# Key-cache gathers in rows of 4 KB instead of 8 KB and 16 KB

## The chip, the cores and the metric

The kernel runs on one core of a Trainium2 chip. The metric is the device time of one execution in microseconds (us). Before the change the median of 5 runs is 1200.76 us (1194.84 to 1205.26). One more execution was recorded by the hardware profiler: it took 1201.02 us, of which 1199.2 us lie between its first and its last instruction (the span). All steps are worked out from that execution.

## The reference, cut to what matters

Four layers are added to `x` (64 sequences of 64 tokens, 512 wide, float32), each with a residual. The third is attention over a paged key and value cache; it holds everything that the change touches. For sequence `b`, token `t` stands at position `pos = kv_lens[b] + t`, and sees the 256 positions up to its own:

```
blk = take_along_axis(block_tables, pos // 16, axis=1)
k_blocks = k_blocks.at[blk, :, pos % 16, :].set(k)      # blocks of [4 heads, 16 positions, 64]
k_all = k_blocks[block_tables]                          # per sequence: its blocks in order
scores = einsum('bghtd,bgsd->bghts', qg, k_all) * SCALE
allowed = (kpos <= pos) & (kpos > pos - 256)
p = softmax(where(allowed, scores, -inf)); o = einsum(p, v_all); out = o @ Wo.T
```

`qg` are the queries, 2 heads to each of the 4 key heads. The new keys are written into blocks of the shared cache before they are read, and the block tables are drawn at random, so a block that one sequence writes may be read by others. The first layer multiplies each sequence by its own 64x64 matrix, the second and fourth are linear layers with low-rank adapters by sequence.

## The kernel before

**What a sequence needs.** A sequence's window touches at most NR = 21 blocks of 16 positions. The kernel takes four sequences at a time: 4 x 21 = 84 blocks, one block to a partition. There are 16 such quadruples, `q` = 0 to 15.

**Two sources of a key block.** Blocks come first from the cache as it was (`kblk`, 16 KB a block, stored head by head: [4 heads, 16 positions, 64]), and then blocks that the kernel itself has written are put over them. The written blocks lie in a scratch tensor `pk` in HBM, 320 rows of 16 KB, stored position by position ([16 positions, 4 heads, 64]); the first stage fills it through `put_rows` (scatters at line 71). `ik_old` and `ik_new` (lines 119 and 120 of the kernel, filled in `gather_indices`, lines 573 to 576) hold the row numbers of both, for each of the 84 partitions and 16 quadruples. Where a block was not written, the number in `ik_new` is out of bounds, and the gather leaves the partition as it is.

**The steps of a key block.** All gathers are issued by POOL through the helper at line 65.
- `k_load(q, h)` (line 148): gathers two heads of the 84 cache blocks into `kt`, 8 KB a row; two calls make a quadruple.
- `k_copy(q, o4)` (line 154): ACT or DVE copies every fourth position from `kt` to `k2`, turning the order to position by position. Four calls make a quadruple.
- `k_patch(q)` (line 161): one gather of 16 KB rows from `pk` over `k2`.
- `k_turn(q, gp, o4)` (lines 169 to 184): PE transposes the positions `4*oq + o4`, oq = 0 to 3, of two heads into one PSUM bank (line 175); DVE or ACT copies it to `kT_mem` (lines 183, 184). Eight calls make a quadruple.

**Values.** `v_load(b)` issues four gathers of 92 rows of 1 KB into `vs_mem`, `v_copy(b)` copies them on ACT into `vt_mem` (line 197), `v_patch(b)` gathers written blocks over them (92 rows of 4 KB, bounded), and `v_share(b)` moves some of the rows by three DMAs from SP (line 208).

**The stages.** In the first stage (to about 450 us) the tokens go through layers one and two, keys, values and queries are made, and the new rows are scattered; the last quarter of the queries is left for the second stage. The second stage has 128 steps, 8 for a quadruple: two for each sequence, one for each half of the heads (`gp`). The order on every engine is the order of the program, written out by hand. A round of 8 steps (`i = s % 8`) issues on POOL: at even `i` four value gathers for sequence b+3; at odd `i` the value patch for b+2, which waits for that sequence's `v_copy` at the end of the step before; at `i` = 1 the key patch of the next quadruple; at `i` = 2 and 3 the cache gathers of the one after it. PE makes the first `k_turn` of the next quadruple at the end of step 3 and the other seven in steps 4 to 7. `k_copy` for the quadruple after it runs at `i` = 5, 6, 7 on DVE and at `i` = 0 of the next round on ACT. In the first round POOL also normalizes the queries that were left over (lines 242, 243, 248), and PE transposes them (line 283). Line 1059 is the product with Wo, lines 1067 to 1086 the fourth layer, line 983 the scores, line 1025 the transposes of the probabilities, line 1041 the product with the values.

Before the second stage, at `n == NTILE`, the program issues `k_patch(0)`, `v_patch(0)` and `v_patch(1)` on POOL, and query products of POOL behind them; `k_load(0, .)` and `k_load(1, .)` stand among the scatters of the first stage.

```
if i == 1:
    k_patch(q + 1)
if i in (2, 3):
    k_load(q + 2, i - 2)
```

Of the kernel before, what the change touches and what calls it, by code (L numbers as in the profile page):

```python
# [11 lines left out]
I32 = mybir.dt.int32  # L12
AF = mybir.ActivationFunctionType
ALU = mybir.AluOpType
# [4 lines left out]
P = 128  # L19
B, T, D = 64, 64, 512  # L20
# [3 lines left out]
NB_TAB = 257  # L24
# [3 lines left out]
NH, NG = 8, 4  # L28
# [3 lines left out]
NR = 21  # L32
NW = 5
W0 = NR - NW
NWR = B * NW
# [15 lines left out]
def kernel(  # L51
# [9 lines left out]
    V, S, G, PE, DMA = nc.vector, nc.scalar, nc.gpsimd, nc.tensor, nc.sync  # L61

    def gather(dst, src, idx, bound=None):
        more = {} if bound is None else dict(bounds_check=bound, oob_is_err=False)
        G.indirect_dma_start(  # L65
            out=dst, out_offset=None, in_=src,
            in_offset=bass.IndirectOffsetOnAxis(ap=idx, axis=0), **more,
        )
# [10 lines left out]

    k_halves = kblk.rearrange("n (h g) o d -> (n h) (g o d)", h=2)
    k_rows = kblk.rearrange("n g o d -> n (g o d)")
    v_blocks = vblk.rearrange("n g o d -> n (g o d)")
    v_rows = vblk.rearrange("n g (q o) d -> (n g q) (o d)", q=4)
# [2 lines left out]
    pk = dram.tile([NWR, ROW], F32, name="pk", tag="pk")  # L88
# [4 lines left out]
    def ctile(shape, dt, name, pool=const):  # L93
        return pool.tile(shape, dt, name=name, tag=name)
# [14 lines left out]
    woT_sb = ctile([P, 4, D], F32, "woT_sb")  # L109
# [6 lines left out]
    cen = ctile([P, B], F32, "cen")  # L116
    edge = ctile([P, 1], F32, "edge")
    lowb = ctile([P, B], F32, "lowb")
    ik_old = ctile([4 * NR, 2, 16], I32, "ik_old")
    ik_new = ctile([4 * NR, 16], I32, "ik_new")  # L120
    iv_old = ctile([NV, B, NG], I32, "iv_old")
    iv_new = ctile([NV, B], I32, "iv_new")
    iod_f = iod.rearrange("p o q j -> p (o q j)")
# [7 lines left out]
    kt = ctile([P, NG, BLK, HD], F32, "kt")  # L131
    k2 = ctile([P, BLK, NG, HD], F32, "k2")
# [8 lines left out]
    def bank(pool, name):  # L141
        return pool.tile([P, 512], F32, name=name, tag="b")

    NP = 4 * NR
# [3 lines left out]
    def k_load(q, h):  # L148

        if q < B // 4:  # L150
            gather(kt[:NP, 2 * h : 2 * h + 2].rearrange("p g o d -> p (g o d)"), k_halves,
                   ik_old[:, h, q : q + 1])

    def k_copy(q, o4):

# [2 lines left out]
                k2[:NP].rearrange("p (oq o) g d -> p oq o g d", o=4)[:, :, o4],  # L158
                kt[:NP].rearrange("p g (oq o) d -> p oq o g d", o=4)[:, :, o4])

    def k_patch(q):

        if q < B // 4:
            gather(k2[:NP].rearrange("p o g d -> p (o g d)"), pk, ik_new[:, q : q + 1], NWR - 1)

    def kT(q, gp):
        return kT_mem[q % 2][:, gp].rearrange("p (b o c i) -> p b o c i", b=4, o=3, c=4)
# [46 lines left out]
    def queries(n):  # L214

        return n - LQ if n < NTILE - 4 else -1 if n < NTILE else n - 4 - LQ
# [77 lines left out]
    with ExitStack() as one:  # L294
# [4 lines left out]
        def t1(shape, dt, name):  # L299
            return ctile(shape, dt, name, c1)  # L300
# [41 lines left out]
                        for i in range(2))  # L342
        kvb_i = t1([P, B], I32, "kvb_i")
        kvp_i = t1([P, 1], I32, "kvp_i")
        cond_i = t1([P, B], I32, "cond_i")
        ad1_i = t1([P, B], I32, "ad1_i")
        ad3_i = t1([P, B], I32, "ad3_i")
        tab_i = woT_sb[:, 2, :NB_TAB].bitcast(I32)
        sc1b = t1([P, 4], F32, "sc1b")
        sc3b = t1([P, 8], F32, "sc3b")  # L350
        pcol = t1([P, 1], F32, "pcol")
# [212 lines left out]
        def gather_indices(part):  # L564

            ps = bank(psO, f"ps_idx{part}")
            lhs, rhs, m, n = ((ix["lhs"].rearrange("p b j -> p (b j)"), ix["hi"], 4 * NR, 16)
                              if part < 2 else
                              (ix["lhsv"].rearrange("p c i -> p (c i)")[:, :NV], ident2, NV, B))
            o = ps[:m, :n]  # L570
            PE.matmul(o, lhsT=lhs, rhs=rhs, start=True, stop=True)
            if part == 0:
                for h in range(2):
                    V.tensor_scalar(ik_old[:, h], o, 2.0, float(h), ALU.mult, ALU.add)
            elif part == 1:
                V.tensor_copy(ik_new, o)
            elif part == 3:
                V.tensor_scalar(iv_new, o, 4.0, ix["oq"], ALU.mult, ALU.add)
            else:
                for g in range(NG):  # L580
                    V.tensor_scalar(iv_old[:, :, g], o, 16.0, ix["oqg"][:, g : g + 1],
                                    ALU.mult, ALU.add)
# [212 lines left out]
        def first_parts(s):  # L795

            if s >= NGRP:
                return [lambda: None] * 4

            def part0():  # L800
                for i in range(4):
                    mix(4 * s + i)
                ranks1(s)

            def part1():
                scale1(s)
                layer1(s, 0)

            def part3():
                layer1(s, 2)  # L810
                layer1(s, 3)

            return [part0, part1, lambda: layer1(s, 1), part3]
# [68 lines left out]
        for n in range(NLAST):  # L882
            if n % 4 == 0:
                parts = first_parts(n // 4 + 1)
            w_load0(n + 12)
            x2_load(queries(n + 2))
            if 1 <= n <= NTILE:
                new_rows(n - 1)
            if n != NTILE:
                norm_q(queries(n - 1))()  # L890
            lag = 4 if n < 20 else 3 if n < 22 else 2 if n < 24 else 1
            while done["p"] <= min(n - lag, NTILE - 1):
                put_rows(done["p"])
                done["p"] += 1
            if n == NTILE:
                k_patch(0)
                v_patch(0)
                v_patch(1)
                norm_q(queries(n - 1))()
            product_q(queries(n), psP)  # L900
            if n % 4:
                x_load0(n + 8)
            if n in (14, 16, 18, 20):
                gather_indices((n - 14) // 2)
            if n < NTILE:
                parts[n % 4]()
            if n % 4 == 0:
                x_load0(n + 8)
            if n == 1:
                written_rows()  # L910
                places()
            if n in (1, 2):
                for o4 in (0, 1):
                    fill_copy(2 * (n - 1) + o4)
            if n == 2:
                fill_store(pv)
            if n >= 2:
                winners(n + 1 + max(0, (n - 6) // 4))
            if 2 <= n < 8:
                zero_rows((pk, pv)[n % 2], n // 2 - 1)  # L920
            if n in (13, 15, 17, 19):
                index_lists((n - 13) // 2)
            if n % 4 == 3:
                mixers(n // 4 + 2)
            if 5 <= n < 10:
                late_inputs(n - 5)
            if 14 <= n < 18:
                positions(n - 14)
            if n == 19:
                adapters(ad3_i, sc3b, 8, mask3)  # L930
                middles()
            if n == 21:
                residual3()
                G.memset(sm_mem, 0.0)
            turn_q(queries(n - 5 if n == NTILE else n - 2 if n != NTILE - 3 else -1), psO)
            if n < NTILE:
                product_kv(n)
            if n in (NTILE - 13, NTILE - 12):
                k_load(0, n - (NTILE - 13))
            if n in (NTILE - 11, NTILE - 9):  # L940
                v_load((n - (NTILE - 11)) // 2)
            if n in (NTILE - 7, NTILE - 5):
                v_copy((n - (NTILE - 7)) // 2)
            if NTILE - 8 <= n < NTILE - 4:
                k_copy(0, n - (NTILE - 8))
            if n in (NTILE - 3, NTILE - 2):
                k_load(1, n - (NTILE - 3))
            if n == NTILE - 4:
                v_load(2)
# [167 lines left out]
    for s, (q, b, gp) in enumerate(steps):  # L1117
        i = s % 8
        turn1, turn2 = turns.get(i, (None, None))
        if i == 0 and q:  # L1120
            x_load(q)
        if i == 2:
            q_load(q + 1)
        if gp == 0:
            v_load(b + 3)
        else:
            v_share(b + 1)
            v_patch(b + 2)
        if i == 1:
            k_patch(q + 1)  # L1130
        if i in (2, 3):
            k_load(q + 2, i - 2)
        scores(s + 1)
        turn_p(s)
        if 0 < s < 16:
            turn_q(nq + s - 2, psO)
        if turn1:
            k_turn(q + 1, *turn1)
        maxima(s + 1)
        keep_p(s)  # L1140
        exponentials(s + 1)
        second = norm_q(nq + s if q < 2 else -1)
        if parts:
            parts.pop(0)()
        if q < 2:
            product_q(nq + s + 1, psM)
            x2_load(nq + s + 3)
        shares(s + 1)
        second()
        if gp:  # L1150
            window(b + 2)
        po = values(s)
        if turn2:
            k_turn(q + 1, *turn2)
        keep_o(s, po)
        if gp == 0:
            v_copy(b + 2)
        if i == 0:
            k_copy(q + 1, 3)
        elif i > 4:  # L1160
            k_copy(q + 2, i - 5)
        if i == 7:
            parts += last_parts(q)
# [53 lines left out]
```

## Time and profile before

| what | before |
|---|---|
| median of 5 runs (lowest to highest) | 1200.76 us (1194.84 to 1205.26) |
| the profiled execution | 1201.02 us |
| its span | 1199.2 us |
| granted TensorE clock, mean | 0.976 |
| PE / DVE / ACT / POOL busy | 1100.0 / 753.4 / 571.4 / 614.2 us |
| key patches, `k<-pk,ik_new` | 16, 1.01 us of POOL each |
| cache gathers, `kt<-in_kblk_dram,ik_old` | 32, 0.95 us (median) of POOL each |
| PE's idle time that a key patch ended | 15.0 us in 13 places |

PE is TensorE's matmuls, PEld its weight loads, DVE VectorE, ACT ScalarE, POOL GpSimd, SP SyncE. In a row of the timeline stand the start, the duration, the engine, the line, the operation, what it writes and reads (`out<-in`), the count, and in brackets the engine's idle time before it with what ended that. A gather's row on POOL is the time in which POOL makes its descriptors; when the data has landed is read from the updates of the gather's semaphore, and from whoever waits for it.

### The profile page before, as it was taken

How to read it: one execution, taken by the hardware profiler on the slowest of the kernel's cores; microseconds unless marked ns; L12 is line 12 of the kernel's file. 1: busy time of each engine (PE TensorE's matmuls, PEld its weight loads, DVE VectorE, ACT ScalarE, POOL GpSimd, SP SyncE). 2: the span in 40 equal slices, each digit the busy share in tenths (PEclk: the TensorE clock that was granted, in tenths of full speed). 3: DMA queues.
4: the chain of work that ended last, by engine and by line, in shares of the span. 5: the costliest groups of instructions: out<-in, count | busy, mean ns of one | idle time of the engine just before them, and what ended most of it. 6: DMA issues, size and time to landing. Idle time of an engine off the chain costs nothing.

```text
span 1199.2 us, 17686 instructions
## 1 busy us (share of the span) xinstructions
PE 1100.0 (92%) x5622; PEld 639.2 (53%) x5622; DVE 753.4 (63%) x2313; ACT 571.4 (48%) x1472; POOL 614.2 (51%) x601
## 2 busy tenths in 40 slices
PE   4998899999899986888999989999999999999998
PEld 4444444444444433445566556656656665665665
DVE  3675445756666683797666656666766676666561
ACT  1332222232224333555566656656666665666551
POOL 3153231333362262688666666667656666655620
PEclk9999999999899997898999999999999999999999
DMA  8366623132432364454665556457556755766420
GB/s 261 114 254 225 228 82 99 57 125 81 150 111 78 95 174 117 115 140 130 140 153 149 132 131 157 135 133 167 144 136 151 168 133 138 160 142 138 100 65 36
DMA packets 129821, 163.20 MB, mean 136 GB/s; under 512 B 58080, under 2 KB 96892, under 8 KB 125546
## 3 DMA queue, kind: packets, MB, share of 16 engines
q0 software_dynamic: 63872, 85.04, 29.4%
q1 hardware_dynamic: 46416, 53.89, 14.8%
q10 hardware_dynamic: 19440, 23.15, 5.7%
q8 instruction: 45, 0.74, 0.3%
q14 instruction: 48, 0.39, 0.1%
HBM read 139.66 MB, written 50.33 MB: 158 GB/s over the span
## 4 chain that ended last, share of the span: by engine, by line
PE 61%; DVE 11%; DMA 10%; ACT 5%; issue 5%; POOL 3%; ACTq 1%; SPq 0%; POOLq 0%; DVEq 0%
PE pso L1059 7%; PE pp L1025 6%; PE psc L983 6%; PE po L1041 6%; PE q L263 5%; PE ps L787 5%; PE psy L1084 5%; PE psy L1078 5%; PE kv L820 5%; DMA k<-pk,ik_new 4%; PE psk L175 3%; PE psxa L1067 2%; PE psy L1086 2%; DMA pv<-vt_mem,zidx 2%; PE ps L789 2%
## 5 line engine op out<-in xcount | busy, mean ns | idle before, releaser
L65 POOL DMA_INDIRECT vs_mem<-in_vblk_dram,iv_old x256 | 309.6, 1209 | 78.1 <-issue 67.6
L1009 ACT ACTIVATE sm_mem<-sm_mem,mn 128x336 f32<-128x336 f32 x256 | 145.6, 574 | 32.9 <-DVE mn L999 31.8
L65 POOL DMA_INDIRECT vt_mem<-pv,iv_new x64 | 80.1, 1252 | 135.7 <-ACT vt_mem L197 77.8
L999 DVE CUSTOM_DVE_ANT_0 sm_mem<-psc,pen 128x336 f32<-128x336 f32 x256 | 118.7, 500 | 16.4 <-PE psc L983 14.7
L1059 PE MATMUL pso<-oT,woT_sb 128*128 128x256 f32 x512 | 123.3, 385 | 0.0
L1041 PEld LDWEIGHTS po<-pT,vt_mem 124*64 124x64 f32 x1536 | 82.6, 136 | 75.4 <-ACT sm_mem L1009 54.2
L263 PE MATMUL q<-wq_sb,x2q 128*128 128x512 f32 x256 | 120.3, 615 | 0.0
L983 PE MATMUL psc<-kT_mem,qs 64*128 64x336 f32 x512 | 108.7, 500 | 10.7 <-DVE kT_mem L184 10.7
L787 PE MATMUL ps<-kT_mem,kT_mem 128*128 128x512 f32 x256 | 117.0, 600 | 0.6 <-PE ps_fill L493 0.6
L1041 PE MATMUL po<-pT,vt_mem 124*64 124x128 f32 x1536 | 113.7, 281 | 3.7 <-ACT pT L1032 3.7
L1025 PE MATMUL pp<-ident,sm_mem 128*124 128x128 f32 x768 | 114.0, 284 | 2.3 <-DVE sm_mem L1017 1.6
L1017 DVE TENSOR_SCALAR sm_mem<-sm_mem,rsum 128x336 f32<-128x336 f32 x256 | 110.3, 431 | 9.1
L820 PE MATMUL kv<-wkv_sb,xr 128*128 128x512 f32 x256 | 115.5, 595 | 0.4 <-ACT va L828 0.4
L1025 PEld LDWEIGHTS pp<-ident,sm_mem 128*124 128x124 f32 x768 | 81.8, 140 | 63.6 <-issue 50.5
L248 POOL TENSOR_TENSOR q<-q,rsq 128x512 f32<-128x512 f32 x30 | 31.8, 1062 | 141.0 <-DVE rsq L246 110.3
L1059 PEld LDWEIGHTS pso<-oT,woT_sb 128*128 128x128 f32 x512 | 92.5, 192 | 12.6 <-ACT oT L1049 2.7
L175 PE MATMUL psk<-ident,k 84*128 84x84 f32 x512 | 63.6, 250 | 20.6 <-ACT kT_mem L184 13.8
L787 PEld LDWEIGHTS ps<-kT_mem,kT_mem 128*128 128x128 f32 x256 | 49.0, 192 | 61.6 <-issue 60.4
L263 PEld LDWEIGHTS q<-wq_sb,x2q 128*128 128x128 f32 x256 | 49.8, 199 | 59.1 <-issue 58.9
L1032 ACT COPY pT<-pp 124x384 f32<-124x384 f32 x128 | 61.7, 482 | 33.3 <-PE pp L1025 25.2
L820 PEld LDWEIGHTS kv<-wkv_sb,xr 128*128 128x128 f32 x256 | 47.0, 191 | 57.2 <-issue 55.7
L973 ACT ACTIVATE pen<-pen,edge 128x336 f32<-128x336 f32 x64 | 36.8, 576 | 80.8 <-DVE pen L972 80.8
(223 smaller groups left out, 1786.8 us busy)
## 6 DMA issues: line engine op xcount, KB each, us to landing
xt<-in_x_dram SPq DMA_DIRECT2D x32, 256.0 KB
x2d<-xr SPq DMA_DIRECT2D x8, 1024.0 KB
x2q<-x2d SPq DMA_DIRECT2D x32, 256.0 KB
qd<-qt ACTq DMA_DIRECT2D x64, 128.0 KB
qs<-qd SPq DMA_DIRECT2D x16, 512.0 KB
xq<-x2d SPq DMA_DIRECT2D x16, 512.0 KB
out_dram<-ys ACTq DMA_DIRECT2D x32, 256.0 KB
vt_mem<-vt_mem SPq DMA_DIRECT2D x192, 28.0 KB
```

What stands on the lines that cost most here:

```text
L65: G.indirect_dma_start(out=dst, out_offset=None, in_=src, in_offset=bass.IndirectOffsetOnAxis(ap=idx, axis=0), **more,)
L175: PE.transpose(ps[:, oq, :], k2[:NP, 4 * oq + o4, 2 * gp : 2 * gp + 2].rearrange("p g d -> p (g d)"), ident[:NP, :NP])
L263: PE.matmul(psq[n], lhsT=xt[:, c, :], rhs=wq_sb[:, c, :], start=(c == 0), stop=(c == KC - 1))
L787: PE.matmul(ps, lhsT=wb_sb[:, c, oc * P : (oc + 1) * P], rhs=x1_mem[:, c, :], start=(c == 0), stop=False)
L820: PE.matmul(pskv[n], lhsT=xrs[s][:, c, i * P : (i + 1) * P], rhs=wkv_sb[:, c, :], start=(c == 0), stop=(c == KC - 1))
L983: PE.matmul(pscs[s][g], lhsT=qts[q][gs, gp, b % 4].rearrange("p h t -> p (h t)"), rhs=kT(q, gp)[gs, b % 4].rearrange("p o c i -> p (o c i) ...
L999: V.tensor_tensor_reduce(rows4(sm)[:, :, :, :28], rows4(pscs[s][g]), rows4(pens[b]), SCALE, 3.0e38, ALU.add, ALU.min, mn)
L1009: S.activation(w, w, AF.Exp, bias=mn, scale=-1.0, accum_out=rsum)
L1017: V.tensor_scalar(w, w, rsum, None, ALU.mult)
L1025: PE.transpose(pp[:NVK, o, :], sms[s][g][0][:, o * P : o * P + NVK], ident)
L1041: PE.matmul(po[g * HD : (g + 1) * HD, :], lhsT=vt(b)[:NVK, o, 2 * gp + g], rhs=pTs[s][g][:, o, :], start=(o == 0), stop=(o == 2))
L1059: PE.matmul(o, lhsT=woT_sb[:, c, ec * P : (ec + 1) * P], rhs=oT[:, c // 2, :, c % 2, :], start=(c == 0), stop=(c == 3))
```

## The change

Every key gather now has rows of 4 KB. A cache gather brings one head instead of two: `k_load(q, h)` issues two gathers where it issued one, so a quadruple has four. A patch brings a quarter of the positions instead of all: `k_patch(q, oq)` gathers positions `4*oq` to `4*oq + 3`, and every place that called `k_patch(q)` calls it for oq = 0 to 3 in a row. The index lists grow with it: four lists of cache rows instead of two, four of patch rows instead of one. To make room for them, two small tables of the setup (`cond_i`, `ad1_i`) move into a part of `woT_sb` that is loaded later.

```diff
-    k_halves = kblk.rearrange("n (h g) o d -> (n h) (g o d)", h=2)
+    k_heads = kblk.rearrange("n g o d -> (n g) (o d)")
...
-    ik_old = ctile([4 * NR, 2, 16], I32, "ik_old")
-    ik_new = ctile([4 * NR, 16], I32, "ik_new")
+    ik_old = ctile([4 * NR, NG, 16], I32, "ik_old")
+    ik_new = ctile([4 * NR, 4, 16], I32, "ik_new")
...
         if q < B // 4:
-            gather(kt[:NP, 2 * h : 2 * h + 2].rearrange("p g o d -> p (g o d)"), k_halves,
-                   ik_old[:, h, q : q + 1])
+            for g in (2 * h, 2 * h + 1):
+                gather(kt[:NP, g].rearrange("p o d -> p (o d)"), k_heads, ik_old[:, g, q : q + 1])
...
-    def k_patch(q):
+    def k_patch(q, oq):
 
         if q < B // 4:
-            gather(k2[:NP].rearrange("p o g d -> p (o g d)"), pk, ik_new[:, q : q + 1], NWR - 1)
+            gather(k2[:NP, 4 * oq : 4 * oq + 4].rearrange("p o g d -> p (o g d)"),
+                   pk.rearrange("w (q r) -> (w q) r", q=4), ik_new[:, oq, q : q + 1], NWR * 4 - 1)
...
-        cond_i = t1([P, B], I32, "cond_i")
-        ad1_i = t1([P, B], I32, "ad1_i")
         ad3_i = t1([P, B], I32, "ad3_i")
-        tab_i = woT_sb[:, 2, :NB_TAB].bitcast(I32)
+        tab_i, cond_i, ad1_i = (woT_sb[:, 2, lo : lo + n].bitcast(I32)
+                                for lo, n in ((0, NB_TAB), (NB_TAB, B), (NB_TAB + B, B)))
...
             if part == 0:
-                for h in range(2):
-                    V.tensor_scalar(ik_old[:, h], o, 2.0, float(h), ALU.mult, ALU.add)
+                for g in range(NG):
+                    V.tensor_scalar(ik_old[:, g], o, float(NG), float(g), ALU.mult, ALU.add)
             elif part == 1:
-                V.tensor_copy(ik_new, o)
+                for oq in range(4):
+                    V.tensor_scalar(ik_new[:, oq], o, 4.0, float(oq), ALU.mult, ALU.add)
...
             if n == NTILE:
-                k_patch(0)
+                for oq in range(4):
+                    k_patch(0, oq)
                 v_patch(0)
                 v_patch(1)
...
         if i == 1:
-            k_patch(q + 1)
+            for oq in range(4):
+                k_patch(q + 1, oq)
```

## The prediction

> **What bounds it now.** I read the page first, then the second stage cut into its sixteen rounds of four sequences, then PE's and POOL's rows, then when each gather landed. The page:
>
> ```profile
> PE 1100.0 (92%) x5622; PEld 639.2 (53%) x5622; DVE 753.4 (63%) x2313; ACT 571.4 (48%) x1472; POOL 614.2 (51%) x601
> ...
> PE 61%; DVE 11%; DMA 10%; ACT 5%; issue 5%; POOL 3%; ACTq 1%; SPq 0%; POOLq 0%; DVEq 0%
> ```
>
> PE sets the time; POOL is half busy over the whole span, but not where it matters. Of the DMA's tenth, 4% (48 us) is `k<-pk,ik_new`, the patch of the key blocks. That is the length of the transfers, not of what PE loses: most of it lies beside PE's other work. What is lost is read from the rounds, cut where each patch is issued (one row with a stall, one without; columns: window, length, busy time and count by engine, clock, DMA share, GB/s):
>
> ```profile
> 687.60:732.70 45.10, 41.50 (x269) 27.14 (x268) 27.11 (x92) 26.65 (x73) 27.27 (x24) 0.96 0.57 134
> ...
> 774.10:815.50 41.40, 39.98 (x269) 25.76 (x268) 26.98 (x92) 26.55 (x73) 27.30 (x24) 1.00 0.58 148
> ```
>
> Six of the thirteen windows from 562.8 to 1108.1 are 41.3 or 41.4 us, PE all but full: the unhindered round, 41.35. All thirteen sum to 545.3, that is 7.7 over 13 x 41.35, and 3.7 of it is the one round above. PE's and POOL's rows in it:
>
> ```profile
> 699.27 0.51 PE L175 MATMUL psk<-ident,k 84*128 84x84 f32 x4 [2.49 <-DMA k<-pk,ik_new]
> ```
>
> ```profile
> 686.06 1.23 POOL L65 DMA_INDIRECT vt_mem<-pv,iv_new  x1 [3.38 <-PE pp L1025]
> 687.59 1.01 POOL L65 DMA_INDIRECT k<-pk,ik_new  x1 [0.30 <-issue]
> 688.91 1.21 POOL L65 DMA_INDIRECT vs_mem<-in_vblk_dram,iv_old  x1 [0.31 <-issue]
> ...
> 699.52 1.21 POOL L65 DMA_INDIRECT vs_mem<-in_vblk_dram,iv_old  x1 [0.64 <-DMA k<-pk,ik_new]
> ```
>
> The patch issued at 687.59 landed 11.6 us later, and PE's first key transpose waited 2.5. In a round without a stall the transpose comes 9.1 to 9.3 us after the issue: that is the **deadline**. By the trace's semaphore updates the fourteen patches from 562.8 on landed after 7.4 to 11.6 us, median 9.1, so about half just miss it. The trace's DMA records show why they are long: 33 to 50 packets of 16 KB, 0.9 to 1.3 us each on average, the first 1.7 us after the issue, the last ending at 6.5 to 10. Two more things: an issue costs about 1.0 to 1.2 us plus 0.3, whatever the row's length; and the last row above waited for the landing of the gather eight places before it, whose semaphore it reuses.
>
> **The change, part by part.** Durations from POOL's groups by form:
>
> ```profile
> L65 POOL DMA_INDIRECT vs_mem<-in_vblk_dram,iv_old x256 | 309.6, 1209 | 78.1 <-issue 67.6 <-PE pp L1025 4.0 <-DMA vt_mem<-vt_mem 2.9
> L65 POOL DMA_INDIRECT vt_mem<-pv,iv_new x64 | 80.1, 1252 | 135.7 <-ACT vt_mem L197 77.8 <-PE pp L1025 43.8 <-ACT k L157 4.1
> ...
> L65 POOL DMA_INDIRECT kt<-in_kblk_dram,ik_old x32 | 31.8, 995 | 9.6 <-issue 8.1 <-DMA vs_mem<-in_vblk_dram,iv_old 1.2 <-PE psk L175 0.3
> ...
> L65 POOL DMA_INDIRECT k<-pk,ik_new x16 | 16.2, 1014 | 6.8 <-issue 4.0 <-DMA pk<-k,sidx 2.3 <-ACT pT L1032 0.3
> ```
>
> The bytes stay. POOL gets 16 x 3 more patch gathers at 1.01 + 0.30 = 1.31 us and 32 more cache gathers at 0.95 + 0.30 = 1.25: 3.93 + 2.50 = 6.43 us a round, 103 in all. A gather of 84 rows costs 0.95 at 8 KB and 1.01 at 16 KB, so I take the same at 4 KB.
>
> POOL's round now is 16 value gathers x 1.50 + 4 value patches x 1.54 + 1.31 + 2 x 1.3 = 34.1 us; with 6.43 more it is 40.5 of 41.35. It fits, with 0.8 to spare, because the 104 us that POOL waits for ACT L197 and PE L1025 ahead of the value patches in these rounds (8 a round) are the cover. It does not fit at the seams. Working through what moves:
>
> (a) Start of the second stage. The first patch stands ahead of two value patches and of the query product that PE waits for:
>
> ```profile
> 451.93 1.03 POOL L65 DMA_INDIRECT k<-pk,ik_new  x1 [2.27 <-DMA pk<-k,sidx]
> 453.26 1.28 POOL L65 DMA_INDIRECT vt_mem<-pv,iv_new  x1 [0.31 <-issue]
> 454.85 1.24 POOL L65 DMA_INDIRECT vt_mem<-pv,iv_new  x1 [0.30 <-issue]
> 456.12 2.04 POOL L248 TENSOR_TENSOR q<-q,rsq 128x512 f32<-128x512 f32 x2
> ```
>
> ```profile
> 457.23 1.11 PE L283 MATMUL pst<-ident,q 128*128 128x128 f32 x4 [10.11 <-POOL q L248]
> ```
>
> POOL runs back to back and PE has been idle for 10 us: three more issues are **+3.9**, uncovered. The cache gathers at 432.8 and 436.9 stand among scatters that wait for each other's landings; 1.25 us each, 0 to 2.5, I take **+0.7** (the scatter behind them waits 3.0 us for a landing anyway).
>
> (b) The first round, 487 to 550, where POOL also normalizes queries: no idle but the issue gaps. Its query products end 1.6 us (fourth), 2.5 and 2.3 us (fifth, sixth) before PE transposes them; ahead of the fourth stand 3.93 + 1.25 more, ahead of the fifth and sixth 6.43. PE loses 5.2 - 1.6 = 3.6, then 0.5 more: **+4.1**. About 1 us of lateness is left and makes the next round's patch late: **+0.7**.
>
> (c) The patch in thirteen full rounds. The transposes at line 175 read positions 4*oq+o4 of all four quarters, so PE waits for the last, issued 3.93 later. Its own landing no row shows. Lower end: value gathers, at the least 3.9 us. Upper end: value patches that stand behind key gathers, median 8.5. The nearest row is the value patch with plain traffic ahead: also 4 KB rows and a bounds check, the same patched blocks; median 5.8. So the last quarter lands at 9.7, 0.6 behind the deadline, and the longer wait list adds some 0.1 of 51 ns waits: 0.7 x 13 = 9.1 come, 7.7 go: **+1.4**. By the ends: -7.7 (landing at 7.8, no stall) and, at 12.4, 3.3 a round, +35; I cut that to +16, since the three quarters ahead are lighter than the key gathers that make the 8.5.
>
> (d) Everything behind the patch on POOL is late: value gathers 3.9, the value patch at step 3 by 5.2, the last cache gather by 6.4, then back to zero by the next patch. Covers: value gathers land 5 to 7 us before ACT copies them (line 197); the step-3 value patch lands about 9.5 before PE needs it, of which SP's three sharing DMAs take some 4.5; the cache blocks land 4 us (1.0 to 7.5) before DVE's copy at line 157, and the last, half as big, should land 2 sooner after its issue. All just covered; where the cover is short DVE or ACT stands still for 1 or 2 us, part of it hidden (DVE is 65% busy). I take 0.1 a round: **+1.5**, 0 to +20.
>
> (e) Nothing: five more 84x16 conversions on DVE (0.12 to 0.16 each, at 225 and 252, beside PE); two index rows that now lie in `woT_sb` and are read hundreds of instructions before its load.
>
> **Sum:** 3.9 + 0.7 + 4.1 + 0.7 + 1.4 + 1.5 = 12.3 on the profiled execution's 1201.0 (span 1199.2), so **1213 us**; the median of the runs, 1200.8, is 0.2 lower.
>
> The Trainium skill speaks against this change: "DMA: Bandwidth & Descriptors", "Rules for kernel authors", wants many small transfers coalesced into one large one. Its "Anatomy of one DMA" gives a price, 2.0 us plus bytes at 436 GB/s; for 35 rows of 16 KB that is 3.3 us, and this trace measured 9.1, so the row disagrees. By that price a quarter lands 2.3 us after its issue, the last at 6.3, no round would stall, and the sum would be about 1204.
>
> **Rivals.** *The patch gets shorter* (0.20): its packets are a quarter as long and spread over four issues; if the last quarter lands within 5.2 us, (c) is -7.7 and (a), (b) remain: 1203, within 0.5% of no change. For it: value gathers land in 3.9. Against: value patches of the same rows take 5.8.
>
> *POOL is the bound* (0.25): 0.8 us of spare is little. If its round reaches 43 (gathers 6% longer, or a wait for the gather eight before in each round), all 14 rounds run at that: 14 x 1.05 over the mean of 41.95 now, and (a), (b): 1225. Deciding point: its round above 41.35. For it: POOL's rows come to 98%; against: no row shows a gather getting slower when POOL is full.
>
> *Faster* (0.06): (c) at -7.7 and the seams covered by PE's own lateness: 1193. Against: PE's 10 us of idle in (a).
>
> The forecast has 0.49. 0.5% is about what a measurement of this kernel tells from no change: faster 0.06, same 0.20, slower 0.74. The range, 1199 to 1232, leaves out the fastest case and the worst of POOL's.
>
> **What would show it.** PE's idle at 457 rises from 10.1 to 14; the fourth to sixth query transposes wait for POOL; POOL busy near 690 us with 78% in the middle rounds; the idle before line 175 that the patch ended stays near its 15 us. Wrong, if rounds drop to 41.35, or if value patches on POOL never wait and rounds pass 42.5.

## The result, and the profile after

The changed kernel takes 1206.28 us (median of 42 runs, 1199.4 to 1214.45) against 1200.6 us (79 runs) of the kernel before. The ratio is 1.0049, with a 95% interval of 1.0036 to 1.0062: slower by 5.9 us, where the prediction had 12. The profiled execution took 1204.18 us, its span is 1202.4, its clock 0.972.

The page after, busy time by engine and the chain of waits (lines of the code are one or two further down than before: the patch transposes are at 176, the query transposes at 284):

```profile
PE 1101.1 (92%) x5622; PEld 640.6 (53%) x5622; DVE 754.6 (63%) x2318; ACT 572.2 (48%) x1472; POOL 693.7 (58%) x681
...
PE 62%; DVE 11%; DMA 6%; issue 6%; ACT 6%; POOL 5%; ACTq 1%; SPq 0%; POOLq 0%; DVEq 0%
```

POOL is 79.5 us busier for 80 more gathers, PE only 1.1. In the chain the DMA share went from 10% to 6%, POOL's from 3% to 5%: something was won at the transfers and something lost on POOL.

The loss is where the prediction put it. POOL's rows at the start of the second stage, then PE's (start, duration, ..., idle time before it and its end):

```profile
450.70 1.03 POOL L65 DMA_INDIRECT k<-pk,ik_new  x1 [1.76 <-DMA pk<-k,sidx]
...
454.67 1.00 POOL L65 DMA_INDIRECT k<-pk,ik_new  x1 [0.30 <-issue]
455.98 1.24 POOL L65 DMA_INDIRECT vt_mem<-pv,iv_new  x1 [0.30 <-issue]
457.53 1.24 POOL L65 DMA_INDIRECT vt_mem<-pv,iv_new  x1 [0.30 <-issue]
458.80 2.05 POOL L249 TENSOR_TENSOR q<-q,rsq 128x512 f32<-128x512 f32 x2
```

```profile
459.91 1.12 PE L284 MATMUL pst<-ident,q 128*128 128x128 f32 x4 [13.38 <-POOL q L249]
```

```profile
524.19 1.12 PE L284 MATMUL pst<-ident,q 128*128 128x128 f32 x4 [5.29 <-POOL q L249]
```

From the first patch's issue to the query product are 8.10 us, before 4.19. PE's idle time there rose from 10.11 to 13.38, and at the fourth query transpose of the first round from 1.24 to 5.29. Its row before:

```profile
519.21 0.63 PE L283 MATMUL pst<-ident,q 128*128 128x128 f32 x4 [1.24 <-issue]
```

The gain is in the rounds (window, length, busy time by engine, clock, DMA share, GB/s):

```profile
611.40:652.80 41.40, 39.86 (x268) 25.71 (x266) 27.22 (x92) 26.40 (x72) 31.87 (x29) 1.00 0.55 145
...
694.20:735.60 41.40, 39.84 (x268) 25.68 (x267) 27.31 (x92) 26.37 (x72) 31.97 (x28) 1.00 0.57 145
```

POOL is busy 32 of 41.4 us, before 27.3; with the 0.30 us of issue ahead of each of its 28 gathers that is 40. It still waits 1.29 us for PE ahead of one value patch in each round, before 3.38. Cut at the patches' issues, eleven of the thirteen rounds are 41.64 to 41.76 us, one 41.00 and one 42.06; none has a stall such as the 3.7 us of the round at 687.6 before. PE's waits for a key patch, 15.0 us in 13 places, are 0.9 us in 3. That row adds up the matmuls and the weight loads, which wait side by side; the matmuls alone (us in total, times, longest) read before

```profile
PE psk L175 <- DMA k<-pk,ik_new: 6.6, 5, 2.5
```

and now

```profile
PE psk L176 <- DMA k<-pk,ik_new: 0.3, 1, 0.3
```

The span cut at the issue of the first patch of a quadruple, for the profiled executions (us). The last column is the median, over thirteen rounds, from the patch's (or first quarter's) issue to the landing of its last data, and the rounds in which that is over 9.15, about PE's deadline:

| kernel | to the first patch | first to third patch | thirteen rounds | last landing, late rounds |
|---|---|---|---|---|
| before | 451.9 | 110.9 | 545.3 | 9.07, 5 |
| changed | 450.7 | 119.4 | 541.4 | 8.31, 3 |
| changed, `r_after` | 451.7 | 117.5 | 540.7 | 8.54, 0 |
| `r_quarters` | 453.3 | 118.1 | 548.7 | 8.09, 0 |
| `r_heads` | 450.9 | 113.7 | 537.9 | 8.65, 3 |
| `r_empty` | 456.2 | 119.9 | 546.4 | 7.65, 0 |
| `s_heads_empty` | 450.5 | 118.5 | 548.7 | 8.49, 5 |
| `s_seams` | 451.5 | 109.8 | 542.5 | 8.35, 1 |

### The profile page after: what moved, and what is told of

Read it like the earlier page. It is cut to its first block, busy times and chain, and to the rows that moved or that the text cites. A ratio compares the mean times of both kernels' runs of the same rounds, so it can differ in the third digit from the quotient of the medians.

```text
span 1202.4 us, 17890 instructions
## 1 busy us (share of the span) xinstructions
PE 1101.1 (92%) x5622; PEld 640.6 (53%) x5622; DVE 754.6 (63%) x2318; ACT 572.2 (48%) x1472; POOL 693.7 (58%) x681
## 4 chain that ended last, share of the span: by engine, by line
PE 62%; DVE 11%; DMA 6%; issue 6%; ACT 6%; POOL 5%; ACTq 1%; SPq 0%; POOLq 0%; DVEq 0%
PE pso L1061 9%; PE po L1043 6%; PE pp L1027 6%; PE psc L985 6%; PE ps L788 5%; PE kv L821 5%; PE psy L1086 5%; PE psy L1080 5%; PE q L264 5%; PE psk L176 3%; PE psxa L1069 2%; PE psy L1088 2%; DMA pv<-vt_mem,zidx 2%; PE ps L790 2%; DVE pen L974 1%
## 5 line engine op out<-in xcount | busy, mean ns | idle before, releaser
L65 POOL DMA_INDIRECT vt_mem<-pv,iv_new x64 | 82.9, 1295 | 43.6 <-PE pp L1027 19.5
L65 POOL DMA_INDIRECT k<-pk,ik_new x64 | 64.5, 1007 | 21.0 <-issue 10.7
```

The lines of the kernel that those rows point to most:

```text
L65: G.indirect_dma_start(out=dst, out_offset=None, in_=src, in_offset=bass.IndirectOffsetOnAxis(ap=idx, axis=0), **more,)
```

## The experiments

The first theory after the result: the last quarter lands sooner than a whole patch because its rows are short, which ends the stalls (-7.7); POOL's added issues cost 7 us at the start and 0.3 us a round. Rivals: the single-head gathers end the stalls; or the value gathers that now come 3.9 us later do, whatever the patch's rows.

### A set on a chip that makes gathers dear

Four kernels went first, and they fell on a chip on which the kernel before takes 1236.84 us. Their edits are cut to the lines that matter, those of `e3_empty` against the kernel before, the others against the changed kernel.

`e1_quarters`, patches by quarters, cache gathers by two heads as before:

```diff
-            for g in (2 * h, 2 * h + 1):
-                gather(kt[:NP, g].rearrange("p o d -> p (o d)"), k_heads, ik_old[:, g, q : q + 1])
+            gather(kt[:NP, 2 * h : 2 * h + 2].rearrange("p g o d -> p (g o d)"), k_halves,
+                   ik_old[:, h, q : q + 1])
```

> The patches by quarters, the cache gathers by two heads as before. Theory (quarters end PE's stalls, and what the change costs is POOL's extra issues at the start of the second stage and in its first round): the last quarter lands about 8.2 us after the first issue, PE waits for patches under 2 us in all (15 before), rounds of 41.4 to 41.6; the seam costs 3 us at the first patch and 3.93 - 1.6 = 2.3 in the first round. Sum 5.5 - 7.7 + 1.5 = about -1 us: 1199 to 1201, a ratio of 0.998 to 1.001. Rival (the rounds got shorter because cache gathers of single heads load the DMA queue less): patches still make PE wait 10 us or more, ratio 1.004 or more.

`e2_heads`, the other half of the change, patches whole:

```diff
-            for oq in range(4):
-                k_patch(q + 1, oq)
+            k_patch(q + 1)
```

> The cache gathers by single heads, the patches whole. Theory (quarters end the stalls): patches land as before, median about 9, PE's waits for them stay at 10 to 18 us; two more issues at 1.25 us each in a round are covered, and in the first round 1.25 and 2.5 us of lateness stand against 1.6 and 2.5 of room, about +0.5. Sum +0.5 to +2: ratio 1.000 to 1.002. Rival (single heads shorten the rounds): PE's waits for patches under 3 us, rounds of 41.4, ratio 0.994 to 0.996.

`e3_empty`, the kernel before with three gathers more behind each patch, all of whose row numbers are out of bounds:

```diff
             gather(k2[:NP].rearrange("p o g d -> p (o g d)"), pk, ik_new[:, q : q + 1], NWR - 1)
+            for t in none:
+                gather(t, pk.rearrange("w (q r) -> (w q) r", r=16), ik_none, NWR - 1)
```

> The kernel before, with three gathers behind every patch whose indices are all out of bounds: they cost POOL its issue time and move no rows. It has the patch's issue cost without its shorter rows. Theory (shorter rows end the stalls, issues cost at the seams): the whole patch lands at about 9 us as before, PE's waits for it stay at 10 to 18 us, the seams cost 3 + 2.3 us, DVE pays 0.1 to 0.2 us a round: +5 to +8 us, ratio 1.004 to 1.007. Rival (the patch lands sooner in the changed kernel only because the value gathers that stood right behind it are issued 4 us later): patches land at 8 us or less, waits under 3 us, ratio 0.997 to 1.001.

`e4_seams`, the changed kernel with whole patches for the first two quadruples and two-head cache gathers for the first three:

```diff
+        if q < 2:
+            if oq == 0:
+                gather(k2[:NP].rearrange("p o g d -> p (o g d)"), pk, ik_whole[:, q : q + 1], NWR - 1)
+        elif q < B // 4:
...
+        if q < 3:
+            gather(kt[:NP, 2 * h : 2 * h + 2].rearrange("p g o d -> p (g o d)"), k_halves,
+                   ik_half[:, h, q : q + 1])
+        elif q < B // 4:
```

> The changed kernel with the change undone at the seams alone: the patches of quadruples 0 and 1 whole, the cache gathers of quadruples 0, 1 and 2 by two heads; from then on as changed. Theory (the seams cost 7 us, the rounds gain 4): the first key patch of the third round is issued at about 563 as before, rounds of 41.6, ratio to before 0.996 to 0.998. Rival (the loss is a lower granted clock through the whole of the second stage, or POOL's fuller rounds, and not the seams): ratio 1.002 to 1.005, like the changed kernel.

Measured: 1360.89 us for `e1_quarters`, ratio 1.0932 [1.0850, 1.1014]; `e2_heads` 1316.91, 1.0661 [1.0608, 1.0714]; `e3_empty` 1355.44, 1.0975 [1.0911, 1.1039]; `e4_seams` 1394.98, 1.1288 [1.1223, 1.1352]. Every expectation missed by 60 us and more, for all theories alike. PE's rows show no wait for a patch in any of the four, so the loss is another one, and without the changed kernel beside them the four can't be read. The next set has it.

### The two halves, and the quiet alone

The changed kernel as a control, and three of the kernels above under new names. The kernel before takes 1198.3 us on this chip.

> The changed kernel itself, as a control for the three kernels beside it: the four runs before it were made on a chip on which the kernel before took 1237 us, and can't be read against 1200 and 1206. If this chip is an ordinary one: 1206 against 1200.6 of the kernel before, ratio 1.005, PE's waits for a key patch about 1 us in all. If it is like the other chip, the ratio here says what that chip makes of this change as a whole, and the other kernels are read against it: a ratio near 1.005 leaves the four runs before as they stand, a ratio near 1.1 says that they show the chip and not their edits.

Measured: 1206.11 us, ratio 1.0063 [1.0036, 1.0089]. This chip agrees with the result, and the kernels beside it can be read.

> Half of the change: patches by quarters, cache gathers by two heads as before. Theory (the last quarter lands about 1 us sooner after the first issue than the whole patch, so the 7.7 us of stalls in the thirteen rounds go; the added issues cost at the seams and 0.1 to 0.3 us a round): stalls -7.4, seams about +5.5 of the 7.3 of the whole change, rounds +2: within 2 us of the kernel before, 1199 to 1202.5. Rival, the single-head cache gathers are what ended the stalls: the stalls stay, 1207 or more, and PE's waits for patches stay near 15 us.

Measured: 1213.82 us, ratio 1.0117 [1.0072, 1.0162]. Neither: the stalls at the patch are gone, yet the median is above the whole change's. PE's waits in it and two places of its timeline, with the value patch on POOL that stands behind the first cache gather (us in total, times, longest):

```profile
PE po L1043 <- DMA vt_mem<-vt_mem: 3.4, 5, 1.6
...
PE po L1043 <- DMA vs_mem<-in_vblk_dram,iv_old: 1.3, 2, 0.9
```

```profile
917.69 1.26 POOL L65 DMA_INDIRECT vt_mem<-pv,iv_new  x1 [0.30 <-DMA vs_mem<-in_vblk_dram,iv_old]
```

```profile
932.98 0.44 PE L1043 MATMUL po<-pT,vt_mem 124*64 124x128 f32 x4 [0.90 <-DMA vs_mem<-in_vblk_dram,iv_old]
934.97 0.79 PE L1043 MATMUL po<-pT,vt_mem 124*64 124x128 f32 x8 [1.55 <-DMA vt_mem<-vt_mem]
```

PE now waits for values. The value patch of step 3 is issued 12.5 us after the key patch (8.6 before) and takes 8.5 us to land behind a gather of 8 KB rows, so it lands 21.0 us after the key patch's issue where it was 17.4; SP's three sharing DMAs come behind it. By the updates of their semaphores the last of the three lands 27.1 us after the key patch's issue (median over thirteen rounds, at most 30.1), before 23.9, in the changed kernel 26.2. PE's product with these values stands at 26.7 to 26.8 in a round without a stall. This is term (d) with its cover gone: with quarters alone the stalls move from the key patch to the values.

The round with the two rows above takes 47.30 us, 5.8 over the unhindered 41.53 of this kernel, though these waits are 2.45. Behind them the matmuls run slower (four of line 985 take 1.49 us at 937.10, else 0.84). Here are 14 us of that round, and 10 us of the round at 687.6 of the kernel before, around its wait of 2.49 (window, length, busy time by engine, clock, DMA share, GB/s).

```profile
931.00:945.00 14.00, 10.88 (x51) 5.80 (x49) 5.45 (x19) 4.96 (x13) 8.43 (x7) 0.76 0.32 83
```

```profile
696.00:706.00 10.00, 7.51 (x41) 5.67 (x42) 4.32 (x15) 3.32 (x12) 7.14 (x6) 0.83 0.92 197
```

The granted clock is 0.76 and 0.83 there and 1.00 in the rounds without such a wait. So one long wait cost these rounds more than its own length: the 3.7 us of the round at 687.6 hold 2.5 of waiting.

> The other half: cache gathers by single heads, patches whole. Theory: the patch stays as long as before, so the stalls stay (PE's waits for patches near 15 us), and POOL's 2.5 us a round cost 1 to 2 us in the first round: 1201 to 1204. Rival, the single heads end the stalls: 1194 to 1197, PE's waits for patches under 3 us.

Measured: 1193.81 us, ratio 0.9965 [0.9935, 0.9995]: about the rival's time, but not quite its reason, since PE still waits for patches:

```profile
PE psk L175 <- DMA k<-pk,ik_new: 3.9, 5, 1.4
```

In the kernel before, this line reads 6.6 us, 5 times, longest 2.5. The rounds are 7.4 us shorter in sum, the way from the first to the third patch 2.8 longer. The landings by position in the round (median over thirteen rounds, us after each one's issue) show what single heads do:

| gather | before | `r_heads` | `r_quarters` | changed |
|---|---|---|---|---|
| key patch, or its first and last quarter | 9.07 | 8.65 | 4.1, 4.2 | 6.6, 4.4 |
| first, fourth value gather behind the patch | 8.0, 4.8 | 7.6, 5.1 | 4.0, 3.9 | 4.3, 4.0 |
| first, last cache gather | 8.0, 9.4 | 4.8, 5.4 | 7.9, 9.2 | 4.6, 5.5 |
| value patch of step 3 | 8.8 | 6.3 | 8.5 | 6.6 |
| first value gather behind the cache gathers | 8.5 | 4.6 | 8.1 | 5.3 |

In these medians what follows a gather of long rows lands late. The whole patch does so to four value gathers, the two-head gathers to a value patch and four value gathers; two single-head gathers in place of each take 2.5 to 4 us off the first ones behind. How much of the 7.4 us each of these landings is worth was not tried apart.

> The kernel before with three gathers more behind each whole patch; all their row numbers are out of bounds, so they bring nothing and only cost POOL the time to make them. What is behind the patch on POOL is as late as with quarters, the patch itself is whole. Theory (the quarters' shorter landing is what ends the stalls): the stalls stay and the seams are paid, 1205 to 1210, PE's waits for patches 10 us or more. Rival (the patch lands sooner because the value gathers behind it come about 4 us later and leave it the queues): the median landing of the whole patch falls from 9.1 to under 8, the waits to under 4 us, and the time is that of the quarters alone, 1199 to 1202.5.

Measured: 1211.82 us, ratio 1.0093 [1.0063, 1.0123], a little above the first theory's band; but its reason falls. The whole patch lands at a median of 7.65 us, never over 8.83, and PE never waits for it. The rival's mechanism is right and its time is wrong. In the rounds the reason is that of the quarters, PE's waits for values:

```profile
PE po L1045 <- DMA vt_mem<-vt_mem: 1.8, 3, 0.8
...
PE po L1045 <- DMA vs_mem<-in_vblk_dram,iv_old: 0.6, 1, 0.6
```

The last sharing DMA lands at 27.5 us here (median), and the thirteen rounds take 6.1 us more than 13 x 41.56, the unhindered round. The larger part lies ahead of the rounds: the first patch comes 4.3 us later than in the kernel before (the clock of this execution is 0.968), and the third another 9.0 later, where the rival had put 5.5 for the start.

So a whole patch with no rows behind it for 3.9 us lands sooner (7.65) than four quarters do in the same place (8.09). In this kernel short rows are not needed to end the stalls; the pause is enough.

### Whole patches in the changed order, and the start

Next came kernels made from these. `r_heads_empty` is `r_heads` with the three empty gathers: as many gathers as the changed kernel has, in the same order, with patches of 16 KB rows. `r_heads_late` is `r_heads` with two-head gathers for the first three quadruples, and `r_late_one` is that with one empty gather behind each patch from the fourth on:

```diff
+            for t in none if q > 2 else []:
+                gather(t, pk.rearrange("w (q r) -> (w q) r", r=16), ik_none, NWR - 1)
```

> Cache gathers by single heads and the patch whole, with three gathers behind it that bring nothing (all row numbers out of bounds): the gathers of the changed kernel in the same number and order, only that the patch's rows are 16 KB and not 4 KB. New theory (what ends the patch stalls is that the value gathers behind the patch come 3.9 us later and leave it the queues, not its shorter rows): the patch lands at a median under 8.0 us, PE hardly waits for it, and the time is that of the changed kernel, 1203 to 1208. Rival (the 4 KB rows matter): patch stalls as in the kernel before in most rounds, 1210 or more.

> The changed kernel, but the first two quadruples are patched whole and the first three quadruples' cache gathers bring two heads, as before the change; only the steady rounds have the new gathers. Theory (the added gathers cost 7 us between the first and the third patch, where POOL also makes the queries, and win 4 us in the thirteen rounds): 450 to 563 us as in the kernel before, 7 us less than the changed kernel, so 1196 to 1200, ratio 0.996 to 1.000. Rival (the loss is elsewhere: in a lower clock or in the rounds): 1202 or more.

> Whole patches, cache gathers by single heads from the fourth quadruple on. Single heads everywhere took 1193.8 with 2.8 us lost between the first and the third patch against the kernel before. Theory: those come back and the rounds keep their gain, 1189 to 1193, ratio about 0.993. Rival (the gain of single heads stems from the first loads): back at 1196 or more.

> As the kernel with single heads from the fourth quadruple on, and one gather that brings nothing behind each patch from the fourth on: a third of the quiet, 1.3 us, at a third of the lateness. Theory: the patch lands some 0.4 us sooner (a third of the 1.0 to 1.4 us that three of them win), the few stalls left (3 to 4 us in all) go, 1187 to 1192. Rival (any further lateness on POOL costs as much as the stall that it saves): no gain, 1191 to 1196.

These four fell on the first set's chip again (before: 1233.02 us): `r_heads_empty` 1397.83, ratio 1.1315 [1.1259, 1.1371]; `r_seams` 1391.94, 1.1259 [1.1206, 1.1312]; `r_heads_late` 1325.2, 1.0724 [1.0671, 1.0777]; `r_late_one` 1332.68, 1.0657 [1.0585, 1.0729]. All missed. Two of them ran once more on another chip (before: 1200.75):

> The same kernel as r_heads_empty, which ran on a chip where the kernel before takes 1233 us and every kernel with more gathers 1300 to 1400, so that its question stayed open. New theory (the quiet of 3.9 us behind the patch ends its stalls, not its 4 KB rows): the whole patch lands at a median under 8.0 us, PE hardly waits for it, and the time is that of the changed kernel, 1203 to 1208. Rival (the 4 KB rows matter): stalls in most rounds, 1210 or more.

Measured: 1213.26 us, ratio 1.0091 [1.0059, 1.0123]. The time is the rival's, and neither reason fits: the median landing is 8.49, above the theory's 8.0, and five rounds are late, not most. PE's waits:

```profile
PE psk L179 <- DMA k<-pk,ik_new: 4.5, 5, 1.4
PE po L1045 <- DMA vt_mem<-vt_mem: 4.0, 1, 4.0
```

The single wait of 4.0 is for a sharing DMA that was issued at 610.62, 0.50 us behind the whole patch, and landed with it, at 618.44 (the patch at 618.40). That round takes 46.8 us, 5.1 over the unhindered 41.7.

The difference to `r_empty` is ahead of the patch. There POOL waits 3.4 us for PE before the value patch that precedes the key patch, and the last value gather has landed before the next key patch is issued (at 40.2 us of a round of 41.9, medians); here, as in the changed kernel, POOL waits 1.3, and it lands behind that issue (41.9 of 41.7). That this is what makes the patch late again is argued; no run changes it alone. Under those conditions quarters were late in three rounds of one execution and in none of the other, the whole patch in five. So the pause alone does not end the stalls in the changed kernel's order, and what the 4 KB rows add there is not settled: the 3 us that they would be worth lie inside the intervals.

> The same kernel as r_seams, for the same reason: the changed kernel with the gathers of before at the start of the second stage. Theory: 7 us less than the changed kernel, 1196 to 1200, and 450 to 563 us as before. Rival (the loss is in the rounds or the clock): 1202 or more.

Measured: 1196.97 us, ratio 0.9960 [0.9940, 0.9981], as the theory said. The two places of PE's timeline are back:

```profile
456.77 1.11 PE L293 MATMUL pst<-ident,q 128*128 128x128 f32 x4 [10.03 <-POOL q L258]
```

```profile
515.77 0.66 PE L293 MATMUL pst<-ident,q 128*128 128x128 f32 x4 [2.27 <-POOL q L258]
```

From the first to the third patch it takes 109.8 us, the kernel before 110.9 and the changed one 119.4; the rounds keep 2.8 of their gain of 3.9. The start is what makes the change a loss. Part of the gain here goes with the granted clock, whose median is 0.980 in these runs and 0.9765 in those of the kernel before beside them; at 0.976 and 8 us for 0.01, as worked out under "The sum" below, they are 1199.0 and 1201.3.

### Once more, with the changed kernel beside

> The changed kernel again, beside the next one on the same chip. On an ordinary chip 1204 to 1208, ratio 1.004 to 1.007. On a chip where the kernel before takes 1233 us and more: if this ratio is near 1.13, such a chip makes every added gather dear, and the eight runs made there say nothing of their edits.

> The changed kernel's gathers in number and order, with whole patches of 16 KB rows and three empty gathers. The run before gave 1.0091 [1.0059, 1.0123] and key patches that landed over 9.1 us after their issue in five of thirteen rounds. Theory (with gathers close ahead of the patch, whole rows still land late now and then, quarters hardly): 3 us or more above the changed kernel, 1208 to 1213, and three or more rounds with a late patch against at most two of the changed kernel's. Rival (the rows make no difference, and the five late ones were chance): within 2 us of it.

> The same kernel as r_heads_late, which ran on the chip that makes added gathers dear: whole patches, single heads from the fourth quadruple on. Single heads everywhere gave 0.9965, with 2.8 us lost between the first and the third patch. Theory: these come back, ratio 0.992 to 0.996, 1190 to 1195. Rival (the gain comes from the first loads): 0.9975 or more.

> The same kernel as r_late_one: the last one, with one empty gather behind each patch from the fourth on. Theory: the patch lands some 0.4 us sooner than in the kernel with single heads (8.65), the stalls left go, 1187 to 1193. Rival (1.3 us of lateness costs as much as the stalls it saves): no gain over single heads alone.

This set fell on another dear chip, on which the kernel before takes 1243.66 us. `t_after`: 1414.64 us, ratio 1.1358 [1.1281, 1.1435]; `t_heads_empty` 1418.22, 1.1435 [1.1357, 1.1512]; `t_heads_late` 1341.45, 1.0783 [1.0719, 1.0848]; `t_late_one` 1356.8, 1.0904 [1.0838, 1.0971]. The changed kernel itself is 14% slower there, so the totals on such chips say nothing of these mechanisms. Whether 4 KB rows of the patch are worth anything beside the pause stays open, and so does what `r_heads_late` and `r_late_one` take on a chip like the result's.

## Why the prediction was wrong, by its steps

The time fell between the forecast and the rival *The patch gets shorter*; slower came true, with half the size.

**(a) and (b), the start: right in place, mechanism and nearly in size.** The first patch came 1.2 us earlier than before, so the +0.7 for cache gathers among scatters is not seen. The three issues delay the query product by 3.9 us as said, and PE's idle time grew by 3.3 there (to 13.4; 14 was named) and by 4.1 at 524 (4.1 forecast). The third patch is issued at 570.1, before at 562.8: +7.3, where the terms gave 3.9 + 0.7 + 4.1 = 8.7; the +0.7 of (b) behind it, lateness of the next round's patch, is not seen either. `s_seams` takes these issues back, and the time goes from above the kernel before to below it.

**(c), the failed step: the landing of the last quarter.** The prediction took 5.8 us for its own landing, from value patches as the nearest row, and so kept the stalls and added 1.4. It was 4.4 (median), near its lower end of 3.9; the last data landed 8.3 us after the first issue and not 9.7. The stalls went: the rounds are 3.9 us shorter in sum although an unhindered one is 0.27 longer, so the term is about -3.9 - 13 x 0.27 = -7.4, where +1.4 was put down and -7.7 was its lower end. That is 8.8 of the roughly 9 us by which 12.3 was too much on the profiled executions; the start was 2.1 too high and (d) 2.0 too low. The value patches were a poor likeness, and not only behind long rows: the three with plain traffic ahead land in 5.6 to 5.8 us in the kernel before (medians by position) and still in 5.4 to 6.0 in `r_heads` and `r_quarters`, while a quarter takes 4.1 to 4.4 and a value gather with plain traffic ahead as little as 3.9. What makes a value patch the longer was not tried.

The reason given for the rival whose size this term took, shorter packets, is not needed for it: `r_empty` has the old packets and lands at 7.65, by the pause behind the patch. In the changed kernel's own order it is not enough to have the pause, as `s_heads_empty` shows with 8.49 and five late rounds, so there the share of the shorter rows stays open.

**(d), lateness behind the patch: covered in the changed kernel, and thin.** 1.5 was put down; the unhindered round went from 41.38 to 41.65, 3.5 in thirteen. Two places of a round make it: PE's idle time ahead of a key transpose is 0.44 us where it was 0.30, and one group of twelve products with the values (line 1043) takes 1.10 where it took 0.97; what delays them was not tried. A transfer is late for PE's values in one place, by 0.6 us. `r_quarters` shows how thin that is: without single heads the same lateness reaches PE, and the rounds take 548.7. The prediction saw that the value patch of step 3 would be issued 5.2 us later and had a cover of 9.5, of which the sharing DMAs take 4.5; it didn't see that the second half of the change is what keeps that cover. With it the patch lands in 6.6 us instead of 8.8, and the last sharing DMA at 26.2 us, 0.6 ahead of PE's product at 26.8; without it at 27.1.

**POOL as the bound: no.** POOL still waits for PE in each round, 1.29 us with 0.30 of issue in it.

**The sum.** On the profiled executions +7.3 at the start and -3.9 in the rounds make +3.4, and they differ by 3.2. The medians differ by 5.7. From execution to execution, time goes with the granted clock, some 8 us for 0.01: a line through the changed kernel's runs of the result gives 8.7, through those of `r_after` 7.0, through the 24 of the kernel before beside `r_after` 9.1. Set to a clock of 0.976 by 8 us, `r_after` is about 1204.7 and the kernel before beside it 1200.6, +4.1. The rest goes with a lower granted clock, in the median 0.976 in `r_after` and 0.980 in the kernel before beside it (0.974 in the changed kernel's runs of the result); why it is lower is not shown.

The Trainium skill's price in "DMA: Bandwidth & Descriptors", "Anatomy of one DMA", gives an estimate of 2.3 us for a quarter. Measured were 4.1 to 4.4. By it no round would stall, which nearly came true; the price itself did not hold.

## What to carry to other kernels

A gather's landing depends on its neighbours in the queue as well as on its own bytes (a whole key patch took 7.65 us in `r_empty`, a quarter 4.1 in `r_quarters`; a value gather of one size landed after 3.9 us or 8.5), so look at the landings by position in the round, not only at the row that stalls: here long rows two steps later set the cover for what a cut patch makes late. Issues added to an engine are nearly free in the round where it has slack (five more gathers made a round 0.27 us longer) and are paid almost in full where it runs back to back (7.3 us of the 8.7 put down); keep the old form for the first rounds (`s_seams`, 0.9960 where the change is 1.0049). When one half of a change is tried alone, expect either sign: quarters alone cost 1.2%, single heads alone won 0.35% (the interval ends at 0.05%), on one chip.

## What the runs showed of the hardware

The same program is not equally dear on every chip. On two of the four chips of these runs the kernel before takes 1233 to 1244 us instead of 1198 to 1201, and added gathers cost some 2.1 to 3.8 us each: `t_after` 171 us for 80 gathers, `e2_heads` 80 for 32, `e3_empty` 119 for 48 that move no rows, `t_heads_late` 98 for 26. So it is no fixed price for a gather. Beside `r_after` the whole change costs 8 us. A value gather takes POOL 1.19 us in the rows below, about the 1.21 of the kernel before. What is different is that PE, ACT and DVE stand still together, here in `t_heads_late`:

```profile
686.22 0.57 ACT L979 ACTIVATE pen<-pen,edge 128x336 f32<-128x336 f32 x1 [2.90 <-DVE sm_mem L1023]
...
689.22 2.66 SPq L213 DMA_DIRECT2D vt_mem<-vt_mem  x3
689.32 1.19 POOL L65 DMA_INDIRECT vs_mem<-in_vblk_dram,iv_old  x1 [0.30 <-issue]
690.81 1.19 POOL L65 DMA_INDIRECT vs_mem<-in_vblk_dram,iv_old  x1 [0.30 <-issue]
693.49 0.38 ACT L188 COPY kT_mem<-psk 128x252 f32<-128x252 f32 x1 [6.70 <-remote]
693.53 0.51 DVE L1005 CUSTOM_DVE_ANT_0 sm_mem<-psc,pen 128x336 f32<-128x336 f32 x1 [7.35 <-remote]
...
694.04 0.57 PEld L180 LDWEIGHTS psk<-ident,k 84*128 84x128 f32 x4 [7.91 <-ACT kT_mem L189]
694.04 0.82 PE L180 MATMUL psk<-ident,k 84*128 84x84 f32 x4 [7.67 <-ACT kT_mem L189]
```

For 6.7 us no compute engine runs, while POOL and SP go on; "remote" means that the profile finds no releaser in the kernel. After 560 us there are 8 such pauses of over 1.5 us in this execution, 42 us in all, and none in those of the kernel before, `r_after` and `r_heads`. They account for part of the loss; shorter waits of one engine and a lower clock in the profiled executions (0.90 to 0.94, against 0.97 to 0.98) go with them. What causes them, and why on these chips, was not found.
